# Attention with bias: adding and taking the row maximum in one VectorE instruction, and another order of matmuls in the product with v

## The chip, the cores and the metric

The kernel runs on one core of a Trainium2 chip (trn2), whose engines are TensorE (PE), VectorE (DVE), ScalarE (ACT), GpSimd (POOL) and the DMA engines, fed here by SyncE's queue (SP). Each engine works through a queue of its own in order and waits on semaphores that other engines raise. The metric is the device time of one execution in microseconds. All data are fp32.

## The reference, cut to what matters

The program computes four layers on an image of 256 x 256 positions and 128 channels. Each layer is `x = x + layer(group_norm(x))`. The change lies in the first of them, an attention along the rows of the image with 4 heads of 32 channels:

```python
mu = jnp.mean(z_ij, axis=-1, keepdims=True)
var = jnp.var(z_ij, axis=-1, keepdims=True)
z = (z_ij - mu) * jax.lax.rsqrt(var + LN_EPS) * ln_gamma + ln_beta
q = heads(z @ Wq)
k = heads(z @ Wk)
v = heads(z @ Wv)
bias = z @ Wb
g = jax.nn.sigmoid(heads(z @ Wg))
scores = jnp.einsum('bijhd,bikhd->bijkh', q, k) / np.sqrt(C_HIDDEN)
scores = scores + bias[:, None]
a = jax.nn.softmax(scores, axis=-2)
o = jnp.einsum('bijkh,bikhd->bijhd', a, v)
o = (g * o).reshape(b, n, n, HC)
return o @ Wout
```

So for each of the 256 image rows and each head there is a 256 x 256 matrix of scores (queries by keys). The same bias, which depends on query, key and head but not on the row, is added to each of them, and the softmax runs over the keys. The other layers are a selective scan over 65536 positions (by far the longest), a Fourier layer and a gated recurrence.

## The kernel before

`program` calls the layers one after another; each waits for what the one before has left in DRAM. `layer0` first normalises x (lines 110 to 142), leaves z and the bias in DRAM, and then calls `attention` (line 147), which the change edits.

`attention` works in blocks of 2048 positions, that is 8 rows of the image, 32 blocks in all. A block has 16 **units**: a unit is one row with two of the four heads (`u`, with `hp = u % 2` for the pair of heads), 512 units in all. The whole bias stays in SBUF (line 162). For one unit the steps are these:

- `scores` (line 201): four matmuls on PE (line 207), two heads times two halves of the queries, into the PSUM tile `l0b_sc`, of 128 partitions (queries) by 2 heads by 2 halves by 256 keys, which has two buffers. The heads lie in different groups of 32 partitions of q and k, and the loop has the halves outside and the heads inside. Then DVE adds the bias to all 1024 columns in one instruction (line 215), which leaves the sum in `l0b_e` in SBUF (four buffers), and takes the negated maximum over the keys for each of the four pieces in a second one (line 222) into `l0b_top`.
- `exps` (line 224): four exponentials on ACT (line 228), one for each piece, with the negated maximum as bias and the sum over the keys as accumulator output `l0b_den`; the reciprocal of the four sums on DVE (line 231); and the multiplication of the whole tile by it on POOL (line 232).
- `transposes` (line 234): eight transposes on PE (line 240), which bring the keys onto the partitions, four for each half of the keys, into `l0b_tp0` and `l0b_tp1`; ACT copies the first half to `l0b_at0` (line 243), DVE the second to `l0b_at1` (line 245).
- `product` (line 247): four matmuls on PE (line 254), two heads times two halves of the keys, which accumulate over the halves into `l0b_op`. Each head writes 32 partitions of its own. The loop has the heads outside and the halves inside.
- `gate` (line 264), once for two units: DVE multiplies by the gate (line 268).
- `out` (line 277), once for four units: a matmul on PE (line 281), then on DVE the addition of x (line 282) and the statistics for the next group norm (line 283).
- `project` (line 181), sixteen times for a block: the matmuls for k, q, v and the gate of the next block (lines 188 and 193), with a copy on DVE (lines 191 and 195) or ACT (lines 197 and 199).

A matmul of fp32 appears in the profile as two MATMUL instructions, a transpose as one.

The order of the work on all engines is written out by hand (`tc.manual_schedule()`, line 288): the loop runs over `u`, and each turn issues the steps of different units:

```python
if u + 2 < N:
    scores(u + 2)
if u + 1 < N:
    exps(u + 1)
if u < N:
    transposes(u)
if 5 <= i and b + 1 < NB:
    project(b + 1, i - 5)
if 1 <= u <= N:
    product(u - 1)
```

In each turn DVE's queue therefore holds, in this order: the gate (every second turn), the addition and maximum of unit u + 2, the reciprocal of unit u + 1, the copy of the transposes of unit u, and then the copies and additions of `project` and `out`, where there are any. The turns 0 to 4 of a block have no projection. The loads of z and x for the next block go through SP's queue (line 176), as does the store of a finished block (line 285).

Of the kernel before, what the change touches and what calls it, by code (L numbers as in the profile page):

```python
# [11 lines left out]
AF = mybir.ActivationFunctionType  # L12
ALU = mybir.AluOpType
AX = mybir.AxisListType
# [132 lines left out]
def attention(c, x, x1, zs, bs, w, stats):  # L147
# [3 lines left out]
    tc, nc = c.tc, c.nc  # L151
# [4 lines left out]
    with ExitStack() as a:  # L156
# [5 lines left out]
        bias = one.tile([P, NH, 2, S], F32, name="l0b_bias")  # L162
# [38 lines left out]
        def scores(u):  # L201
            k, r, hp = blocks[u // UB], u % UB // 2, u % 2
            sc = ps2.tile([P, 2, 2, S], F32, name="l0b_sc")
            for jt in range(2):
                for h in range(2):
                    hs = slice(32 * (2 * hp + h), 32 * (2 * hp + h) + 32)
                    nc.tensor.matmul(  # L207
                        sc[:, h, jt],
                        k["q"][hs, bass.ds(r * S + jt * P, P)],
                        k["k"][hs, bass.ts(r, S)],  # L210
                        start=True,
                        stop=True,
                    )
            e = es[u] = wk.tile([P, 4, S], F32, name="l0b_e", bufs=4)
            nc.vector.tensor_tensor(  # L215
                e,
                sc.rearrange("p h j k -> p (h j) k"),
                bias[:, 2 * hp : 2 * hp + 2].rearrange("p h j k -> p (h j) k"),
                ALU.add,
            )  # L220
            top = tops[u] = wk.tile([P, 4], F32, name="l0b_top")
            nc.vector.tensor_reduce(top, e, AX.X, ALU.max, negate=True)

        def exps(u):
            e, top = es[u], tops.pop(u)
            den = wk.tile([P, 4], F32, name="l0b_den")
            for i in range(4):
                nc.scalar.activation(  # L228
                    e[:, i], e[:, i], AF.Exp, bias=top[:, i : i + 1], accum_out=den[:, i : i + 1]
                )  # L230
            nc.vector.reciprocal(den, den)  # L231
            nc.gpsimd.tensor_tensor(e, e, den[:, :, None].to_broadcast([P, 4, S]), ALU.mult)  # L232
# [14 lines left out]
        def product(u):  # L247
            k, r, hp = blocks[u // UB], u % UB // 2, u % 2
            if hp == 0:
                ops[u // 2] = ps1.tile([P, S], F32, name="l0b_op")  # L250
            for h in range(2):
                hs = slice(32 * (2 * hp + h), 32 * (2 * hp + h) + 32)
                for kt in range(2):
                    nc.tensor.matmul(
                        ops[u // 2][hs],
                        k["v"][:, 2 * r + kt, hs],
                        ats[u, kt][:, h],
                        start=kt == 0,
                        stop=kt == 1,
                    )  # L260
            for kt in range(2):
                del ats[u, kt]
# [27 lines left out]
        for i in range(UB):  # L290
            project(0, i)
        scores(0)
        scores(1)
        exps(0)
        for u in range(N + 3):
            b, i = divmod(u, UB)
            if u >= 3 and u % 2 == 1:
                gate((u - 3) // 2)
            if i == 4 and b + 1 < NB:
                load_block(b + 1)  # L300
# [10 lines that stand above are left out]
            if u >= 5 and (u - 5) % 4 == 0:  # L311
                out((u - 5) // 4)
            if 5 <= i < 10 and b + 1 < NB:
                project(b + 1, i + 6)
# [1152 lines left out]
```

## Time and profile before

| | |
|---|---|
| time before, median of 3 runs (lowest, highest) | 35963.57 us (35957.72, 35963.6) |
| the profiled execution's own time | 35973.5 us |
| its span, first to last instruction | 35971.7 us |
| mean granted clock of TensorE in the span | 0.908 |
| busy in the span: PE, DVE, ACT, POOL | 83%, 89%, 63%, 74% |
| scores of the first unit start, of the last unit end, about | 805.7 us, 3490 us |

The page comes from one profiled execution. Engines are PE (matmuls), PEld (loading of weights), DVE, ACT, POOL and SP. A line such as `L215 DVE TENSOR_TENSOR` names the line of the kernel and the engine; behind it stand the tile written and, after the arrow, the tiles read. In a group of instructions follow the shapes, the number of instructions, the busy time in us and the mean duration of one in ns, and behind a second bar the idle time of the engine just before them, with what ended it. In the timeline each line has the start in us, the busy time in us, engine, line and operation, and in brackets the idle time before it. A table of stretches gives, for a window of time, each engine's busy time, the clock that PE was granted (1.00 is full), the share of the DMA engines in use and the bytes moved. In the list of waits a line says which engine and line waited for which, for how long in total, how often, and the longest. Matmuls are pipelined and their ends are modelled.

### The profile page before, as it was taken

The page shows a single profiled execution, that of the slowest core. Times are in us where ns is not written, and L with a number is a line of the kernel's source. Part 1 is how long each engine was busy: PE and PEld are TensorE (multiplying, and loading weights), DVE is VectorE, ACT ScalarE, POOL GpSimd, SP SyncE. Part 2 cuts the span into 40 slices and gives each one's busy share as a digit, 9 for nine tenths or more (in the row PEclk, how much of TensorE's full clock was granted, in tenths as well). Part 3 has the DMA queues.
Part 4 walks back from the last instruction along what each step waited for, and adds up shares of the span by engine and source line. Part 5 has one row for each costly group of instructions (what it writes and reads, how often), then busy time and mean ns, then how long its engine had stood idle before and what let it go on. Part 6 is the DMA issues. An engine that isn't in the chain of part 4 may idle for free. (4 is left out here: it accounts for less than half of the span.)

```text
span 35971.7 us, 251006 instructions
## 1 busy us (share of the span) xinstructions
PE 29891.5 (83%) x72562; PEld 12305.1 (34%) x72562; DVE 31866.8 (89%) x21006; ACT 22790.4 (63%) x47086; POOL 26745.5 (74%) x6540
## 2 busy tenths in 40 slices
PE   7888978888888888888888888888888887777988
PEld 1444433333333333333333333333333332223444
DVE  5777989999999999999999999999999998542599
ACT  2555567777777777777777777777777775332476
POOL 1333069999999999999999999999999997210000
PEclk8999989999999999999999999999999998889887
DMA  3111655555555554555555555555555556765211
GB/s 120 39 39 40 150 177 191 191 191 191 191 191 191 191 190 191 191 191 191 196 201 201 201 201 201 201 202 201 201 201 201 201 202 177 147 152 142 73 34 33
DMA packets 2480963, 5947.46 MB, mean 165 GB/s; under 512 B 1412999, under 2 KB 1694360, under 8 KB 1891286
## 3 DMA queue, kind: packets, MB, share of 16 engines
q1 hardware_dynamic: 2479574, 5931.39, 46.6%
q8 instruction: 572, 9.37, 0.1%
q14 instruction: 817, 6.69, 0.1%
HBM read 5238.41 MB, written 692.58 MB: 165 GB/s over the span
## 5 line engine op out<-in xcount | busy, mean ns | idle before, releaser
L651 DVE TENSOR_TENSOR_SCAN l1b_h<-l1b_da,l1b_state,l1b_db 128x1024 f32<-128x1024 f32 x8192 | 18792.8, 2336 | 598.1 <-ACT l1b_db L640 586.8
L666 POOL TENSOR_TENSOR l1b_hc<-l1b_h,l1b_cc 128x2048 f32<-128x2048 f32 x4096 | 18452.2, 4530 | 326.4 <-DVE l1b_h L651 321.0
L685 PE MATMUL l1b_y<-l1b_hc,ident 128*128 128x512 f32 x32768 | 16055.9, 639 | 1122.0 <-POOL l1b_hc L666 1121.9
L636 ACT ACTIVATE l1b_da<-l1b_dl,l_A 128x512 f32<-128x512 f32 (+1 forms) x16384 | 11297.0, 690 | 3153.0 <-DVE l1b_h L651 2845.2
L685 PEld LDWEIGHTS l1b_y<-l1b_hc,ident 128*128 128x128 f32 x32768 | 6525.3, 205 | 10692.9 <-issue 8161.7
L618 POOL TENSOR_TENSOR l1b_db<-l1b_bb,l1b_dus 128x2048 f32<-128x2048 f32 x1536 | 6969.5, 4537 | 1244.8 <-DMA l1b_bb<-l1b_bc 1244.8
L618 DVE TENSOR_TENSOR l1b_db<-l1b_bb,l1b_du 128x2048 f32<-128x2048 f32 x2048 | 4658.3, 2275 | 35.2
L640 ACT ACTIVATE l1b_db<-l1b_state,l1b_db,l1b_af 128x1 f32<-128x1 f32 x8192 | 3047.5, 372 | 0.0
L557 PE MATMUL l1b_mm<-l1b_xd,l_dtw 41*128 41x512 f32 x2048 | 1372.6, 755 | 1706.9 <-ACT l1b_dus L607 1701.2
L583 PE MATMUL l1b_mm<-l1b_tail,ident 128*128 128x512 f32 x2048 | 1293.9, 718 | 1387.1 <-ACT l1b_tail L577 1387.1
L662 ACT COPY l1b_state<-l1b_h 128x4 f32<-128x4 f32 x4095 | 790.3, 193 | 2433.0 <-DVE l1b_h L651 2432.9
L232 POOL TENSOR_TENSOR l0b_e<-l0b_e,l0b_den 128x1024 f32<-128x1024 f32 x512 | 969.8, 1894 | 1777.6 <-DVE l0b_den L231 1461.3
L869 POOL TENSOR_TENSOR l1c_y<-l1c_y,l1c_sz 128x512 f32<-128x512 f32 x256 | 369.8, 1468 | 1346.0 <-ACT l1c_y L866 1345.7
L583 PE MATMUL l1b_mm<-l1b_relu,ident 128*128 128x512 f32 x2048 | 1308.5, 728 | 0.0
L557 PEld LDWEIGHTS l1b_mm<-l1b_xd,l_dtw 41*128 41x128 f32 x2048 | 337.6, 206 | 2521.3 <-ACT l1b_dus L607 2124.2
L618 DVE TENSOR_TENSOR l1b_db<-l1b_bb,l1b_mm 128x2048 f32<-128x2048 f32 x512 | 1171.5, 2288 | 18.2 <-ACT l1b_dus L607 0.7
L607 ACT COPY l1b_dus<-l1b_mm 128x512 f32<-128x512 f32 x512 | 300.2, 586 | 1388.2 <-DVE l1b_db L618 1387.8
L228 ACT ACTIVATE l0b_e<-l0b_e,l0b_top 128x256 f32<-128x256 f32 x2048 | 1014.4, 497 | 209.6 <-DVE l0b_den L231 192.6
L399 DVE SCALAR_TENSOR_TENSOR l1a_mm<-l1a_xi,l1a_each,l1a_mm 128x512 f32<-128x512 f32 x1408 | 1046.0, 755 | 58.5 <-issue 12.7
L583 PEld LDWEIGHTS l1b_mm<-l1b_tail,ident 128*128 128x128 f32 x2048 | 377.3, 207 | 2057.7 <-ACT l1b_tail L577 1813.3
L525 PE MATMUL l1b_du<-l1b_xc,l_xproj 128*40 128x512 f32 x2048 | 981.5, 602 | 62.5 <-DMA l_ds<-in_l_ds 58.4
L215 DVE TENSOR_TENSOR l0b_e<-l0b_sc,l0b_bias 128x1024 f32<-128x1024 f32 x512 | 625.4, 1221 | 369.2 <-PE l0b_sc L207 365.9
(253 smaller groups left out, 30461.1 us busy)
## 6 DMA issues: line engine op xcount, KB each, us to landing
l1b_bb<-l1b_bc SPq DMA_DIRECT2D x2048, 1024.0 KB
l1b_cc<-l1b_bc SPq DMA_DIRECT2D x2048, 1024.0 KB
l_y<-l1b_yo SPq DMA_DIRECT2D x256, 1024.0 KB
l1b_xc<-l_xc SPq DMA_DIRECT2D x128, 1024.0 KB
l1b_xc<-l_xct SPq DMA_DIRECT2D x128, 1024.0 KB
l1b_yo<-l_y SPq DMA_DIRECT2D x128, 1024.0 KB
l_xc<-l1a_o SPq DMA_DIRECT2D x64, 1024.0 KB
l_xct<-l1a_ot SPq DMA_DIRECT2D x16, 4096.0 KB
```

The costliest lines, as they stand in the source:

```text
L228: nc.scalar.activation(e[:, i], e[:, i], AF.Exp, bias=top[:, i : i + 1], accum_out=den[:, i : i + 1])
L232: nc.gpsimd.tensor_tensor(e, e, den[:, :, None].to_broadcast([P, 4, S]), ALU.mult)
L399: nc.vector.scalar_tensor_tensor(mm, xis[i][:, r + dy : r + dy + 2, dx : dx + S], each[:, dh, tap : tap + 1], mm, ALU.mult, ALU.add,)
L525: nc.tensor.matmul(du1[:40], w["xproj"][:, dh, k, :], blocks[ch][0][:, dh, cols(ch)], start=dh == 0, stop=dh == 1,)
L557: nc.tensor.matmul(mm, w["dt"][:, chunks[ch][0], dh * P : dh * P + P], xds[ch % 3][0:41], start=True, stop=True,)
L583: nc.tensor.matmul(mm, c.ident, part, start=i == 0, stop=i == 1)
L618: eng.tensor_tensor(db, bbs[g // 2], du[:, None, :].to_broadcast([P, G, CH]), ALU.mult)
L636: nc.scalar.activation(da[:, o + lo : o + hi], dl[:, lo:hi], AF.Exp, scale=w["A"][:, k, dh, n : n + 1])
L640: nc.scalar.activation(first, states[k][:, dh, two : two + 1], AF.Identity, scale=af[:, two : two + 1], bias=first,)
L651: nc.vector.tensor_tensor_scan(h_, a_, d_, states[k][:, dh, one : one + 1], ALU.mult, ALU.add)
L666: nc.gpsimd.tensor_tensor(hc, hs[g], ccs[g // 2], ALU.mult)
L685: nc.tensor.matmul(ys[j % 2], c.ident, hc[:, i], start=False, stop=j // 2 * G + i == 15)
```

## The change

Two things change, both in `attention`.

First, in `scores` the addition over 1024 columns and the maximum over the same are replaced with four instructions of 256 columns, one for each piece (head and half of the queries). Each computes `(scores + bias) * -1`, writes it to `l0b_e`, and writes the minimum of what it wrote, over the keys and started at 3.0e38, to a column of `l0b_top`. The tile thus holds the negated sum, and `l0b_top` still the negated maximum. In `exps` the exponential takes a scale of -1, so that it computes exp(sum - maximum) as before.

Second, in `product` the two loops change places: the halves of the keys are now outside and the heads inside, so that the first half's matmuls of both heads are issued ahead of the second half's.

```diff
             e = es[u] = wk.tile([P, 4, S], F32, name="l0b_e", bufs=4)
-            nc.vector.tensor_tensor(
-                e,
-                sc.rearrange("p h j k -> p (h j) k"),
-                bias[:, 2 * hp : 2 * hp + 2].rearrange("p h j k -> p (h j) k"),
-                ALU.add,
-            )
             top = tops[u] = wk.tile([P, 4], F32, name="l0b_top")
-            nc.vector.tensor_reduce(top, e, AX.X, ALU.max, negate=True)
+            for i in range(4):
+                nc.vector.tensor_tensor_reduce(
+                    e[:, i],
+                    sc[:, i // 2, i % 2],
+                    bias[:, 2 * hp + i // 2, i % 2],
+                    -1.0,
+                    3.0e38,
+                    ALU.add,
+                    ALU.min,
+                    accum_out=top[:, i : i + 1],
+                )
 
         def exps(u):
             e, top = es[u], tops.pop(u)
             den = wk.tile([P, 4], F32, name="l0b_den")
             for i in range(4):
                 nc.scalar.activation(
-                    e[:, i], e[:, i], AF.Exp, bias=top[:, i : i + 1], accum_out=den[:, i : i + 1]
+                    e[:, i],
+                    e[:, i],
+                    AF.Exp,
+                    scale=-1.0,
+                    bias=top[:, i : i + 1],
+                    accum_out=den[:, i : i + 1],
                 )
...
-            for h in range(2):
-                hs = slice(32 * (2 * hp + h), 32 * (2 * hp + h) + 32)
-                for kt in range(2):
+            for kt in range(2):
+                for h in range(2):
+                    hs = slice(32 * (2 * hp + h), 32 * (2 * hp + h) + 32)
                     nc.tensor.matmul(
                         ops[u // 2][hs],
                         k["v"][:, 2 * r + kt, hs],
```

## The prediction

> **What bounds the kernel now.** I first read the busy time by stage, to see how much of the run the change can touch.
>
> ```profile
> core 0: us, PE busy (x) PEld busy (x) DVE busy (x) ACT busy (x) POOL busy (x), PEclk, DMA share, GB/s
> 805.70:3500.00 2694.30, 2327.62 (x14279) 1295.46 (x14278) 1997.59 (x2805) 1479.66 (x4858) 969.84 (x512) 0.95 0.10 36
> ```
>
> All instructions of the diff run in this row, the attention stage (times in us; behind each engine's busy time its number of instructions): 2694 us of 35972, 7.5%. What follows it needs its result and is not edited, so the forecast is the stage's change. In the stage no engine is full: PE 86%, DVE 74%. PE idles 2694.3 - 2327.6 = 366.7 us. The waits of that window say for what (total, times, longest):
>
> ```profile
> POOL l0b_e L232 <- DVE l0b_den L231: 1461.3, 406, 63.0
> ...
> PE l0b_tp L240 <- POOL l0b_e L232: 253.2, 195, 3.7
> ```
>
> Two thirds of PE's idle time is the transposes waiting for POOL's multiplication by 1/den, in 195 of 512 units, 1.30 us each; and POOL in turn waits for the reciprocal on DVE. Groups of the same window add waits of PE for DVE's copies: L193 48.6 (x) and 28.8 (v), L281 30.7 (k), 108 us in all. The timeline of two units shows why the reciprocal is late:
>
> ```profile
> 2002.57 1.21 DVE L215 TENSOR_TENSOR l0b_e<-l0b_sc,l0b_bias 128x1024 f32<-128x1024 f32 x1
> 2002.93 0.59 ACT L243 COPY l0b_at<-l0b_tp 128x512 f32<-128x512 f32 x1 [3.10 <-PE l0b_tp L240]
> ...
> 2003.21 1.06 PE L254 MATMUL l0b_op<-l0b_at,l0b_v 128*32 128x256 f32 x8
> 2003.81 1.22 DVE L222 TENSOR_REDUCE l0b_top<-l0b_e 128x4 f32<-128x1024 f32 x1
> ...
> 2004.20 1.13 PE L207 MATMUL l0b_sc<-l0b_k,l0b_q 32*128 32x256 f32 x8
> 2004.94 0.17 DVE L231 RECIPROCAL l0b_den<-l0b_den 128x4 f32<-128x4 f32 x1
> 2005.03 0.66 DVE L245 COPY l0b_at<-l0b_tp 128x512 f32<-128x512 f32 x1
> ...
> 2005.61 0.41 DVE L268 SCALAR_TENSOR_TENSOR l0b_gated<-l0b_g,l0b_op 128x256 f32<-128x256 f32 x1
> ...
> 2005.93 1.22 DVE L215 TENSOR_TENSOR l0b_e<-l0b_sc,l0b_bias 128x1024 f32<-128x1024 f32 x1
> ```
>
> ACT sat idle for 3.10 us until 2002.93, so the exponentials that the reciprocal at 2004.94 needs had ended by 1999.83. The reciprocal stood in DVE's queue behind the addition and maximum of the *next* unit (2002.57 to 2004.94). POOL starts at 2005.26 for 1.89 us, and PE, done with the scores at 5.33, waits 1.87 us for it until 2007.20. In the other unit of the pair the transposes follow the scores at once.
>
> The third thing is PE's clock. Stretches of 3.4 us around these waits:
>
> ```profile
> 2003.90:2007.30 3.40, 1.53 (x13) 0.78 (x10) 3.37 (x6) 2.08 (x8) 1.89 (x1) 1.00 0.99 311
> 2007.30:2010.70 3.40, 3.40 (x16) 1.96 (x16) 1.88 (x3) 2.38 (x9) 1.90 (x1) 0.51 1.01 424
> 2014.20:2017.60 3.40, 1.78 (x16) 1.33 (x15) 3.37 (x6) 2.25 (x9) 1.90 (x1) 1.00 0.00 0
> 2017.60:2021.00 3.40, 3.40 (x12) 0.95 (x10) 1.66 (x4) 0.42 (x1) 1.89 (x1) 0.50 0.00 0
> 2044.90:2048.30 3.40, 2.33 (x6) 0.74 (x8) 1.62 (x3) 0.04 (x1) 1.09 (x1) 1.00 0.00 0
> 2048.30:2051.70 3.40, 3.40 (x24) 2.05 (x26) 2.33 (x2) 3.40 (x11) 0.00 (x0) 1.00 0.00 0
> ```
>
> A stretch with PE busy for 1.53 or 1.78 us is followed by one at half clock; after 2.33 us the clock stays. The stage's mean of 0.95 thus stands for 0.05 x 2694 = 135 us of lost PE time (rounding +-13).
>
> [...] No DVE row here has such a read; on ACT the trace has it (L228, 188 ns behind each exponential), and DVE's early start it shows: L268 at 2005.61 took 0.41, the next began at 2005.93.[...]
>
> **The change, part by part.** *Removed*, per unit: the addition (1.22) and the maximum (1.22). From the timeline they hold DVE from 2002.57 to 2004.94: 2.37 us.
>
> *Added*: four fused instructions of 256 elements, PSUM plus SBUF. Main part: L268 has the same width and sources, 0.41 us; behind it the next starts 0.32 after (2005.61 to 2005.93). Accumulator read: no row; nearest is the tiny reciprocal, whose successor starts 0.09 after it (2004.94 to 2005.03). So 0.41 each and 4 x 0.41 = 1.64, a saving of 0.73. Ends: the read hidden wholly, 4 x 0.33 = 1.32, saving 1.05; nothing overlapping, 4 x (0.41 + 0.17) = 2.32, saving 0.05; half rate as in the scan L651 (2336 ns against 1221 for 1024, so +0.28 for 256), 4 x 0.69 = 2.76, *costing* 0.39. I take 0.41[...].
>
> On the path: the waits for POOL shorten by the saving, as the chain addition-maximum-reciprocal-POOL-transposes is serial: 195 x 0.73 = 142 us (their mean of 1.30 is well above 0.73). PE's 108 us for DVE's copies shorten too, since they stand behind the same instructions; at most 108, I take 65. In the other units PE is the limit and the saving is worth nothing. Clock: 1.53 + 0.73 = 2.26 and 1.78 + 0.73 = 2.51 are near or above the 2.33 that keeps full speed, so most half-clock stretches go; of 135 us I take 80, since part of that time lies under a wait already counted. Sum 142 + 65 + 80 = 287 us. What is late next is still POOL: 1.87 - 0.73 = 1.14 us remain.
>
> *New holds*: the scores' PSUM tile is now free after 1.64 us instead of 1.2; it has two buffers and is wanted two units on (2010.85 against 2003.8), so 0. Each fused instruction signals by itself; behind it in DVE's queue stand the reciprocal, the copy of the transposes and the gate, all earlier than now. No DMA is moved, and SP's and POOL's queues keep their order.
>
> *Exponentials*: an immediate scale of -1 for an immediate 1: 0. They may start after the first row of four, on an engine 55% busy: 0.
>
> *Product order*: 8 matmuls take 1.06 us (2003.21). L240's 8 of half the width take 1.09, so 256 wide one after another would be near 1.7: the heads already run in pairs. The new order is the one L207 has (1.13 for 8). If pairing broke, 0.8 x 512 = 410 us would be lost, which L207 excludes; not waiting for the second half of the keys could gain at most what the loads of L254 wait for L245, 39 us in the stage. Taken: 0.
>
> **Sum.** The profiled execution took 35973.5 us (span 35971.7): 35973.5 - 287 = 35686.5. The median of the runs is 9.9 lower, so 35677.
>
> **Rivals.** *The read is not hidden* (0.58 each, 2.32): saving 0.05, 10 to 25 us, no change: about 35955. For it: no DVE accumulator read is in the trace. Against: ACT's 188 ns read costs no more than its overlap. *Part of the way* (0.50 to 0.56 each, or half-clock stretches that stay): 100 to 180 us, about 35820. *Slower: [...]*, as L651 does: 2.76 us, +0.39 in every second unit, 256 x 0.39 = 100 us: 36064.[...] It decides from 0.59 us per fused instruction (2.37 / 4). *The change does nothing*, because PE is the limit: against it stand the 253 us.
>
> **How the numbers follow.** The forecast 0.62 (its own range 35590 to 35780), part of the way 0.12, unhidden 0.08, two cycles 0.18. About 0.2% (72 us) is what a measurement tells from no change. Faster 0.74, same 0.08, slower 0.18. The range from 35590 (read hidden, 1.05 saved: about 370 us) to 36000 leaves out the two-cycle case and the little below.
>
> **What would show it.** DVE's four rows from first start to reciprocal near 1.64 us; waits of L240 for POOL from 253 to some 110 us; clock 0.95 to 0.98; the rows of L254 unchanged. I am wrong if a fused instruction takes over 0.55 us from start to start, if POOL then waits for the exponentials, or if the clock stays at 0.95.

## The result, and the profile after

The changed kernel takes **35586.94 us** (median of 4 runs, 35581.59 to 35590.76) against 35963.58 for the kernel before: a ratio of 0.9895, 95% interval 0.9878 to 0.9912, or 377 us less. The forecast was 287 less: the sign and the place were right, the size was too small by 90, and the time lies 3 us below the low end of the range. The profiled execution took 35581.59 us, its span 35579.7.

First the attention stage by time, here from its first scores to its last (us, busy us of each engine, clock of TensorE):

```profile
core 0: us, PE busy (x) PEld busy (x) DVE busy (x) ACT busy (x) POOL busy (x), PEclk, DMA share, GB/s
...
803.50:3107.70 2304.20, 2181.32 (x14219) 1238.98 (x14220) 1527.50 (x5861) 1432.54 (x4845) 964.25 (x510) 1.00 0.11 43
```

Before, the first and the last scores lay 2683.2 us apart; now it is 2304.2, so all of the 377 us is in the stage. PE is busy for 95% of it (2181.3 us, where it was 2319.8), and the clock is at 1.00 where it was 0.95.

The waits in the same stretch as in the prediction, 805.70 to 3500.00 (total, times, longest):

```profile
POOL l0b_e L242 <- DVE l0b_den L241: 764.6, 322, 61.0
...
PE l0b_tp L250 <- POOL l0b_e L242: 74.7, 109, 1.6
...
PE l0b_mm L193 <- DVE l0b_x L292: 48.6, 62, 0.8
```

The transposes' wait for POOL fell from 253.2 to 74.7 us. Of the 108 us that PE waited for DVE's copies, the part for x (48.6) is as it was, and those for v (28.8) and k (30.7) are gone. The groups of the stage show the new instruction (busy us, mean ns, then idle time before it):

```profile
L218 DVE CUSTOM_DVE_ANT_0 l0b_e<-l0b_sc,l0b_bias 128x256 f32<-128x256 f32 x2048 | 745.5, 420 | 418.9 <-PE l0b_sc L207 415.5
...
L218 DVE DVE_READ_ACCUMULATOR2_ANT l0b_top<- 128x1 f32 x2048 | 170.1, 83 | 0.0
```

So an accumulating instruction of DVE is two here: the trace has 420 ns for the main one and 83 ns for the read. What matters is where the read lies, and that only the timeline shows:

```profile
2002.36 0.43 DVE L218 CUSTOM_DVE_ANT_0 l0b_e<-l0b_sc,l0b_bias 128x256 f32<-128x256 f32 x1
2002.71 0.08 DVE L218 DVE_READ_ACCUMULATOR2_ANT l0b_top<- 128x1 f32 x1
2002.71 0.42 DVE L218 CUSTOM_DVE_ANT_0 l0b_e<-l0b_sc,l0b_bias 128x256 f32<-128x256 f32 x1
...
2003.40 0.42 DVE L218 CUSTOM_DVE_ANT_0 l0b_e<-l0b_sc,l0b_bias 128x256 f32<-128x256 f32 x1
2003.74 0.08 DVE L218 DVE_READ_ACCUMULATOR2_ANT l0b_top<- 128x1 f32 x1
2003.74 0.17 DVE L241 RECIPROCAL l0b_den<-l0b_den 128x4 f32<-128x4 f32 x1
...
2004.06 1.89 POOL L242 TENSOR_TENSOR l0b_e<-l0b_e,l0b_den 128x1024 f32<-128x1024 f32 x1 [2.89 <-DVE l0b_den L241]
```

Each read starts in the same moment as the next main instruction (2002.71 and 2002.71; the last one beside the reciprocal, 2003.74); in the whole trace 1955 of the 2048 reads start together with another instruction of DVE. The read adds next to nothing to the chain: from one main instruction to the next it is 0.345 us (median), where L268, of the same width and without a read, was followed after 0.32. From the first start to the reciprocal it is 1.38 us where it was 2.37, a saving of **0.99 us**; the prediction had 1.64 and 0.73.

And the stretches of 3.4 us around these instructions:

```profile
2001.00:2004.40 3.40, 3.40 (x27) 2.62 (x28) 3.06 (x12) 1.39 (x5) 0.51 (x2) 1.00 0.00 0
2004.40:2007.80 3.40, 3.40 (x23) 1.75 (x20) 1.11 (x5) 1.49 (x6) 1.56 (x1) 1.00 0.02 5
...
2014.60:2018.00 3.40, 2.62 (x10) 0.71 (x6) 1.92 (x3) 0.00 (x0) 1.40 (x1) 1.00 0.00 0
```

PE is no longer half idle in any of them, and the clock column stays at 1.00.

**A sum to be tested.** The stage lasts as long as TensorE is busy and idle in it. If its idle time is its waits (for POOL's multiplication and for DVE's copies), and if work done at half clock takes twice as long (in the kernel before, L240's transposes start 109 ns apart at clock 1.00 and 213 ns apart at 0.50), a kernel's difference from before should be the difference in these waits plus half of the difference in the time at half clock (the time in which the trace's record of TensorE's clock says 0.50; the record has the two values 1.00 and 0.50, and in the kernel before all but one of its 2402 entries last a multiple of 3.41 us). Added up between first and last scores, that time is 286.8 us before, 13.7 after; the 13.7 are the first stretch of the stage. Waits: 74.7 + 48.6 - 361.3 = -238. Clock: (13.7 - 286.8) / 2 = -137. Together -375, against a stage that is 379 us shorter. The second term has a figure of its own: PE's busy time fell by 138 us (2319.8 - 2181.3). The prediction gave the same two terms 142 + 65 = 207 and 80.

### The profile page after: what moved, and what is told of

The parts are those of the page before. It is cut to its first block, busy times and chain, and to the rows that moved or that the text cites. A ratio compares the mean times of both kernels' runs of the same rounds, so it can differ in the third digit from the quotient of the medians.

```text
span 35579.7 us, 254592 instructions
## 1 busy us (share of the span) xinstructions
PE 29747.9 (84%) x72562; PEld 12259.8 (34%) x72562; DVE 31402.5 (88%) x24078; ACT 22740.5 (64%) x47086; POOL 26737.3 (75%) x6540
## 5 line engine op out<-in xcount | busy, mean ns | idle before, releaser
L661 DVE TENSOR_TENSOR_SCAN l1b_h<-l1b_da,l1b_state,l1b_db 128x1024 f32<-128x1024 f32 x8192 | 18792.9, 2336 | 596.4 <-ACT l1b_db L650 585.7
L218 DVE CUSTOM_DVE_ANT_0 l0b_e<-l0b_sc,l0b_bias 128x256 f32<-128x256 f32 x2048 | 745.5, 420 | 418.9 <-PE l0b_sc L207 415.5
```

The lines of the kernel that those rows point to most:

```text
L661: nc.vector.tensor_tensor_scan(h_, a_, d_, states[k][:, dh, one : one + 1], ALU.mult, ALU.add)
```

## The experiments

The theory: what delays the stage is what the reciprocal and the copies stand behind in DVE's queue; the waits follow from it, and the clock is a term of its own that is added to them. The rivals are stated with each run. Each ratio is against runs of the kernel before on the same chip.

**The two parts apart.** First the new order in the product alone, on the kernel before:

```diff
-            for h in range(2):
-                hs = slice(32 * (2 * hp + h), 32 * (2 * hp + h) + 32)
-                for kt in range(2):
+            for kt in range(2):
+                for h in range(2):
+                    hs = slice(32 * (2 * hp + h), 32 * (2 * hp + h) + 32)
```

> The kernel before with the new order of matmuls in the product alone; addition and maximum stay two instructions. My theory: the heads already ran in pairs, so nothing beyond 6 ns per unit, 3 us in all: 35960 +-10. The rival, that not waiting for the second half of the keys is where part of the unforecast 90 us came from, has at least 40 us: 35920 or less.

Measured: 35937.47 us (35930.61 to 35944.49), ratio 0.9993, interval 0.9985 to 1.0001: 27 us less than before, with an interval that includes no change, though its 13 runs all lie below those of the kernel before on the same chip (35957.54 and up). The waits did not move:

```profile
PE l0b_tp L240 <- POOL l0b_e L232: 254.5, 196, 3.7
...
PE l0b_mm L193 <- DVE l0b_x L282: 48.6, 62, 0.8
...
PE l0b_mm L281 <- DVE l0b_k L195: 30.6, 32, 1.0
...
PE l0b_mm L193 <- DVE l0b_v L191: 29.0, 31, 0.9
```

The time at half clock fell from 286.8 to 231.5 us, worth 28. That the heads already ran in pairs the trace of the kernel before shows: the matmuls of L254 start two at a time, 13 ns apart (7 ns in the changed kernel's L264), and each pair 216 ns after the last. The order thus saves no wait; fewer stretches fall to half clock (60 instead of 76, without the first and the last 30 us). Why these 16 don't, isn't settled: in the kernel before 45 half-clock stretches follow one with PE 52 to 53% busy, and 8 stretches after such a one keep the clock; with the new order it is 29 and 18.

Then the fused instruction alone, with the old order in the product.

> The changed kernel with the old order of matmuls in the product: the fused instruction alone. My theory: the whole gain, 35587 +-10, since the product order is worth nothing. The rival that the product order carries part of the gain: 35620 or more.

Measured: 35587.01 us (35585.58 to 35589.34), ratio 0.9896, interval 0.9881 to 0.9911: the whole gain. Here 20.0 us of half clock are left, all in one stretch at the start of the stage, so the order of the product has nothing to win any more. The product's matmuls, on which the prediction wanted no change, in this kernel (old order) and in the changed one:

```profile
L264 PE MATMUL l0b_op<-l0b_at,l0b_v 128*32 128x256 f32 x4096 | 545.9, 386 | 0.0
```

```profile
L264 PE MATMUL l0b_op<-l0b_at,l0b_v 128*32 128x256 f32 x4096 | 541.0, 385 | 0.0
```

The same mean. In the kernel before it was 422 ns, with a tenth of the stage at half clock: 385 ns at clock 1.00 and 634 at 0.50.

**Do the exponentials gain from starting early?** The four fused instructions in reverse order, so that the first exponential waits for the last of them:

```diff
-            for i in range(4):
+            for i in (3, 2, 1, 0):
                 nc.vector.tensor_tensor_reduce(
```

> The changed kernel with its four fused instructions in the reverse order, so that the first exponential has to wait for the last of them, as it did for the maximum before. Theory (the exponentials' earlier start is worth nothing): within 12 us of the changed kernel, 35575 to 35600. Rival (part of the gain is that ScalarE may start after the first quarter): the first exponential comes up to 3 x 0.345 = 1.03 us later, and the time rises to 35640 or more.

Measured: 35587.48 us (35580.93 to 35589.03), ratio 0.9897, interval 0.9882 to 0.9912. The time is that of the changed kernel; the rival falls. The early start is there in the changed kernel: in 194 of the 512 units the first exponential starts before the unit's last accumulator read has ended, by up to 1.00 us; the time shows nothing of it.

**How the time follows the delay of the reciprocal.** A memset on DVE between the fused instructions and the reciprocal, of a tile that nobody reads, gives part of the saved time back:

```diff
+        pad = one.tile([P, 330], F32, name="l0b_pad")
...
+            nc.vector.memset(pad, 0.0)

         def exps(u):
```

> The changed kernel with a VectorE memset of 330 columns of a spare tile behind the four fused instructions of each unit, about 0.25 us of the queue, so that the stretch from the first fused instruction to the reciprocal takes the 1.64 us that the prediction had instead of 1.38. Theory 1, the mis-sized term is the saving per unit (the accumulator read costs nothing) and the clock: the two halves of the miss part here. If the prediction's other terms were right, 35677; if the clock term was too small by some 60 us, 35587 + 195 x 0.25 = 35636 or a little more, clock 0.98 or above in the stage. Rival, the gain comes from something else than DVE's time (exponentials that start after one piece of four): 35587 still.

> The changed kernel with a VectorE memset of 650 columns between the fused instructions and the reciprocal: from the two pads run so far, first start to reciprocal about 1.38 + 0.15 + 0.52 = 2.05 us. Theory (the gain has two terms, waits in proportion to that time and a clock that stays full as long as the stretches around the waits are busy enough): waits about half way between the short pad (178 us) and before (361), some 270, so 35656 + 92 = 35750 if the clock stays full, and up to 35880 if it falls back; the half-clock time tells which. Rival (one slope for all): 35656 + 308 x 0.33 / 0.65 = 35812, with half-clock time about half of the 287 us before.

> The same with a memset of 1250 columns, about 1.02 us, which gives back all that fusing saved on DVE's queue (2.37 us again), while the scores' tile is free early and the exponentials may start after one piece. Theory: all of the gain goes, 35960 +-60, half-clock stretches come back, the stage's clock about 0.95. Rival, the early start of the exponentials or the earlier release of the scores' tile is worth something by itself: clearly below 35900.

The first tells whether the prediction's other terms were right once its term for the fused instructions is. Of the middle one a timeline:

```profile
2002.53 0.42 DVE L219 CUSTOM_DVE_ANT_0 l0b_e<-l0b_sc,l0b_bias 128x256 f32<-128x256 f32 x1
...
2003.91 0.08 DVE L219 DVE_READ_ACCUMULATOR2_ANT l0b_top<- 128x1 f32 x1
2004.07 0.60 DVE L229 MEMSET l0b_pad<- 128x650 f32 x1
2004.59 0.12 DVE L243 RECIPROCAL l0b_den<-l0b_den 128x4 f32<-128x4 f32 x1
```

It is 2.06 us from the first start to the reciprocal here; over all units the median is 2.07. The memset doesn't start together with the last read, as the reciprocal did, but 0.16 us later (2003.91 to 2004.07); with 330 and 1250 columns the median of that gap is 0.10 and 0.29 us, which I had not counted. From the memset's own start to the reciprocal's it is 0.25, 0.52 and 1.02 us in the timelines of the three runs. The five points:

| columns of the memset | first start to reciprocal, median us | PE's waits, us | half clock, us | worked out | stage, measured | time, us |
|---|---|---|---|---|---|---|
| none (changed kernel) | 1.38 | 123.3 | 13.7 | -375 | -379.0 | 35586.94 |
| 330 | 1.73 | 178.1 | 20.0 | -317 | -307.8 | 35655.82 (ratio 0.9915, 0.9901 to 0.9928) |
| 650 | 2.07 | 264.9 | 98.8 | -190 | -187.7 | 35773.88 (0.9949, 0.9935 to 0.9964) |
| the kernel before | 2.39 | 361.3 | 286.8 | 0 | 0 | 35963.58 |
| 1250 | 2.69 | 428.8 | 446.1 | +147 | +135.9 | 36104.04 (1.0040, 1.0027 to 1.0052) |

"Worked out" is the difference of the waits plus half that of the half clock, against before. It meets each stage within 12 us. The time isn't straight in the delay: by the column of the stage (the times come from chips on which the kernel before differed by up to 10 us), the first 0.35 us cost 71, the next 0.34 cost 120, the next 0.32 cost 188. The waits grow by 55, 87, 96 and 67 us from row to row; half clock does not move at first and then comes in (14, 20, 99, 287, 446 us).

With 330 columns the delay is near the prediction's (1.73 against 1.64), and yet the time is 21 us below the forecast. The two terms part here: the waits are shorter by 183 us where the prediction had 207, and the half clock, of which only the first stretch of the stage is left, is worth 133 where it had 80. So even with the prediction's own figure for the fused instructions its clock term was too small. With 1250 the delay is longer than before, and so is the time; I expected about the time of before, because I took the memset for 1.02 us more where, with the gap before it, it came to 1.31. This is the place of the prediction's slower rival (2.76 us, forecast +100): 2.69 costs +141. Its direction is right, and its turning point, 2.37 us, fits the points on both sides; its price was one of waits alone (they grew by 67) and had left out the clock, 80 of the 147.

**Is the clock a term of its own?** The kernel before, with four transposes of the identity ahead of the transposes of each odd unit, where PE waits. They write what the real ones overwrite:

```diff
                 tp = ps1.tile([P, 2, 2, P], F32, name=f"l0b_tp{kt}")
+                if kt == 0 and u % 2 == 1:
+                    for d in range(4):
+                        nc.tensor.transpose(tp[:, d // 2, d % 2], c.ident, c.ident)
```

> The kernel before, with four transposes of the identity into the tile tp0 (overwritten at once by the real ones) issued ahead of the transposes of every odd unit, where TensorE waits for GpSimd. Theory (the half clock is a term of its own, set by how little TensorE does in a stretch): the 4 x 0.136 = 0.55 us fit into the waits, of 1.30 us[...] and take most of the 287 us at half clock away, worth 143 at most; units without a wait pay 61 x 0.55 = 33. So 35964 - 80 to 110 = 35855 to 35885, with half-clock time under 60 us. Rival (the clock follows the waits, and a faster TensorE only waits longer for GpSimd): the clock rises, the waits for GpSimd grow as much, and the time is within 20 us of before, or up to 140 longer where the transposes are not hidden.

Measured: 35854.33 us (35849.32 to 35858.35), ratio 0.9970, interval 0.9958 to 0.9982. A kernel that only does more work is 109 us faster. One turn, and its stage:

```profile
2000.78 0.66 PE L240 MATMUL l0b_tp<-ident 128*128 128x128 f32 x4
2001.61 1.09 PE L243 MATMUL l0b_tp<-ident,l0b_e 128*128 128x128 f32 x8 [0.17 <-POOL l0b_e L232]
```

```profile
1500.00:2500.00 1000.00, 915.54 (x5920) 530.58 (x5919) 770.18 (x1085) 572.08 (x1877) 372.86 (x197) 0.99 0.10 39
```

The four stand where PE would have idled, 0.17 us of the wait remain, and the clock is 0.99, where the kernel before had 0.95 in the same stretch. Half clock fell from 286.8 to 54.1 us, worth 116. The sum: waits 220.2 - 361.3 = -141, the added transposes 1024 x 0.136 = +139, clock -116: -118, against a measured -108.3. The rival, that a faster PE only waits longer, falls: the waits plus the added work are as long as the waits were. Four added fp32 transposes in each odd unit thus kept the clock at 0.99, though 11 stretches in which PE was 62 to 63% busy were still followed by half clock.

**Which units matter?** The fused instruction in even units alone, and in odd ones alone (the others keep addition and maximum, and a scale of 1):

```diff
-            for i in range(4):
+            if u % 2 == 0:
+                for i in range(4):
...
+            else:
+                nc.vector.tensor_tensor(...)
+                nc.vector.tensor_reduce(top, e, AX.X, ALU.max, negate=True)
```

> The changed kernel with the fused instruction in even units alone; odd units keep addition and maximum. Theory (only the addition and maximum that stand ahead of a waited-for reciprocal count; transposes wait in odd units, and the reciprocal of an odd unit stands behind the addition and maximum of the next, even unit): nearly the whole gain, 35590 to 35650. Rival (what counts is VectorE's load over all units): half of the gain, about 35775.

> The changed kernel with the fused instruction in odd units alone; even units keep addition and maximum. Theory (as for the even units): little of the gain, 35880 to 35965, with the waits for GpSimd still near 250 us. Rival (VectorE's load over all units): half of the gain, about 35775.

Measured: 35840.25 us (35838.43 to 35853.76), ratio 0.9967, interval 0.9954 to 0.9979, for even; 35833.31 (35800.72 to 35839.7), 0.9961, 0.9948 to 0.9974, for odd. My theory of the even units falls: each gives a third of the gain, where I had forecast nearly all for the even and little for the odd ones. But they give different things. Waits with even units fused:

```profile
PE l0b_tp L259 <- POOL l0b_e L251: 118.8, 171, 2.4
...
PE l0b_mm L300 <- DVE l0b_k L195: 90.0, 93, 1.0
...
PE l0b_mm L193 <- DVE l0b_x L301: 48.6, 62, 0.8
...
PE l0b_mm L193 <- DVE l0b_v L191: 28.9, 31, 0.9
```

and with odd units fused:

```profile
PE l0b_tp L259 <- POOL l0b_e L251: 252.0, 193, 3.5
...
PE l0b_mm L193 <- DVE l0b_x L301: 48.6, 62, 0.8
```

The even units' instructions set the waits for POOL in odd units: the reciprocal of an odd unit stands behind them in the queue. The odd units' instructions set those for the copies of k and v: these stand, in an odd turn, behind the odd unit's instructions, and with those fused the two rows are gone. But the row of POOL (253 to 119) hides a move, which a count of the trace's waits by unit shows. Before, 249 us of it lay in odd units and 4 in even ones. With the even units fused, 10 are left in odd units, and 109 lie in even ones, whose reciprocal still stands behind an unfused odd unit. And PE meets the late copy of k at the output projection more often (93 times instead of 32), so that this row rises from 30.7 to 90.0. Of the 240 us won in odd units, 105 come back as waits for POOL in even units and 59 as waits for k. Half clock is 194.0 and 177.5 us. Worked out -121 and -115, measured -119.5 and -126.7. The two gains add up to 253; the other 124 us come only with both. The rival (half of the gain each, 35775) falls too.

**Would the place in the queue alone do?** The reciprocal put ahead of the next unit's addition and maximum, first in the kernel before, then in the changed one:

```diff
-            if u + 2 < N:
-                scores(u + 2)
             if u + 1 < N:
                 exps(u + 1)
+            if u + 2 < N:
+                scores(u + 2)
```

> The kernel before, with the exponentials and reciprocal of unit u+1 issued ahead of the scores, addition and maximum of unit u+2; nothing fused. Theory (what delays the reciprocal is its place in VectorE's queue behind the addition and maximum of the next unit): the reciprocal of the waited-for units comes up to 2.4 us earlier, the 253 us of waits for GpSimd fall under 100, the half clock goes with them: 35600 to 35750. Rival (the length of the chain addition, maximum, exponentials, reciprocal counts, not the place in the queue; and the additions now stand behind a reciprocal that waits for the exponentials): 35950 or slower than before.

> The changed kernel with the exponentials and reciprocal of unit u+1 issued ahead of the scores and fused instructions of unit u+2. From what that order cost the kernel before (358 us; VectorE's reciprocal waited for ScalarE, with the additions and the copies behind it): slower than the changed kernel, 35700 to 35900. Rival (with the chain 0.99 us shorter the exponentials are done in time, so that the remaining 75 us of waits for GpSimd go): 35500 to 35570.

Measured: 36321.11 us (36312.44 to 36325.99), ratio 1.0099, interval 1.0084 to 1.0114, on the kernel before, 358 us slower. In its timeline:

```profile
2009.63 0.18 DVE L231 RECIPROCAL l0b_den<-l0b_den 128x4 f32<-128x4 f32 x1 [3.88 <-ACT l0b_e L228]
2009.72 1.19 DVE L215 TENSOR_TENSOR l0b_e<-l0b_sc,l0b_bias 128x1024 f32<-128x1024 f32 x1
```

and its waits:

```profile
DVE l0b_den L231 <- ACT l0b_e L228: 767.7, 448, 4.8
...
PE l0b_mm L281 <- DVE l0b_k L195: 196.3, 93, 3.2
...
PE l0b_tp L240 <- POOL l0b_e L232: 121.9, 123, 3.7
```

The reciprocal waits for the exponentials, and DVE's whole queue with it: the next unit's addition starts 0.09 us after it, and the copies come late. PE's waits for POOL are halved, but those for the copies rise by more, and half clock goes to 771.0 us. Waits +92, clock +242: +334, against +357.7. My theory of the place in the queue falls in this form.

On the changed kernel the same edit **gains**: 35539.46 us (35535.69 to 35542.83), ratio 0.9884, interval 0.9868 to 0.9901; beside it on the same chip the kernel with the reversed order, equal to the changed one, took 35587.48. Here I had expected a loss; the time lies where the rival had it.

```profile
DVE l0b_den L241 <- ACT l0b_e L233: 511.4, 329, 3.9
...
PE l0b_mm L193 <- DVE l0b_x L292: 48.6, 62, 0.8
...
PE l0b_mm L291 <- DVE l0b_k L195: 28.5, 62, 1.0
...
PE l0b_tp L250 <- POOL l0b_e L242: 5.2, 10, 1.8
```

DVE still waits for the exponentials, 511 us, so they are not always done in time, as the rival had supposed; but DVE has the time to wait: PE's waits for POOL are 5.2, those for k 28.5. Worked out -412, measured -423.6. That it is the 1 us shorter work per unit that makes room is argued from these rows, not shown by a run of its own.

**What is left, and a faster version.** POOL's multiplication in two, the keys that the first transposes read ahead of the others:

```diff
-            nc.gpsimd.tensor_tensor(e, e, den[:, :, None].to_broadcast([P, 4, S]), ALU.mult)
+            for kt in range(2):
+                ks = bass.ts(kt, P)
+                nc.gpsimd.tensor_tensor(
+                    e[:, :, ks], e[:, :, ks], den[:, :, None].to_broadcast([P, 4, P]), ALU.mult
+                )
```

> The changed kernel with GpSimd's multiplication in two, first the 128 keys that the first four transposes read, then the rest. Theory (what is left of TensorE's waits for GpSimd is the length of the multiplication): the first half ends about 0.95 us earlier, and most of the 75 us of waits go: 35520 to 35560. Rival (each GpSimd instruction has a fixed cost of some tenths of a us, and the second half comes later than the whole did; or TensorE is the limit anyway): 35580 to 35650.

Measured: 35543.98 us (35540.96 to 35549.84), ratio 0.9886, interval 0.9871 to 0.9900.

```profile
L244 POOL TENSOR_TENSOR l0b_e<-l0b_e,l0b_den 128x512 f32<-128x512 f32 x1024 | 1042.9, 1039 | 1289.6 <-DVE l0b_den L241 736.7 <-PE l0b_mm L193 526.8 <-PE l0b_tp L254 26.1
```

```profile
PE l0b_mm L193 <- DVE l0b_x L296: 48.6, 62, 0.8
...
PE l0b_tp L254 <- POOL l0b_e L244: 24.6, 100, 0.8
```

Two halves take 2 x 1.04 = 2.08 us where the whole took 1.89, 0.19 more, but the first is done 0.85 us earlier, and 50 of the 75 us of waits go. This and the exponentials first both beat the changed kernel, by 43 and 47 us. That is little, 0.12 and 0.13%, and the intervals of the ratios to the kernel before overlap; but none of the four runs of either comes near those of the reversed order on the same chip (35580.93 to 35589.03). The two together were not tried; they reach for the same waits.

## Why the prediction was right in kind and too small

- **What bounds the stage**: right. PE's waits for POOL were the largest part of the idle time, and they fell most.
- **"4 x 0.41 = 1.64, a saving of 0.73"**: the first step that failed. The prediction had seen main instructions start 0.32 us apart (2005.61 to 2005.93), and added 0.09 for the accumulator read, an estimate, because the trace of before had none on DVE. Measured is 0.345 from start to start, the read wholly beside the next instruction: 1.38 us, near its low end (1.32). The mechanism, a shorter queue ahead of the reciprocal, was right; the size of the saving was not.
- **"195 x 0.73 = 142 us"**: measured 178.5. With the true saving the product would have been 195 x 0.99 = 193, but 56 of the 195 waits were shorter than 0.99 us, which their mean of 1.30 hid; when each wait loses 0.99 us at most, they lose 179.
- **"At most 108, I take 65"**: measured 59.5, and near by luck: the 65 had no working, and at about the saving that the prediction had (the run with 330 columns) the copies give 44. The waits for x stayed whole.
- **"In the other units PE is the limit and the saving is worth nothing"**: wrong. Fusing the odd units alone gains 130 us, through the copies and the clock, and without it two thirds of what the even units win come back as waits for POOL and for k.
- **"Of 135 us I take 80, since part of that time lies under a wait already counted"**: the second step that failed, and with 57 us the larger error. Waits and clock don't overlap, they add: the half clock comes in the stretch after the half-idle one, in which PE is busy and each matmul takes longer (L254: 634 ns where it takes 385 at full clock). The prediction's own rows showed PE busy for 3.40 of 3.40 us in both of its stretches at half clock. Nearly all of it went, (286.8 - 13.7) / 2 = 137 us. The run with added transposes shows it as a term of its own (116 us for no shorter chain), and the run with 330 columns shows it gone at 0.66 us of saving already (133 us).
- The errors add up: 287 + 36 (waits for POOL) - 6 (copies) + 57 (clock) = 374, against 375 from the sum above and 377 measured.
- **Product order 0, exponentials' start 0, new holds 0**: right beside the fused instruction (35587.01 without the new order, 35587.48 with the exponentials held). Alone the order is worth perhaps 27 us through the clock, a way that the prediction had not seen. The 410 us for broken pairs don't follow from the prediction's own figures (1.7 - 1.06 = 0.64 us a unit, or 330; the 1.7 was an estimate, which the 216 ns from pair to pair bear out, 8 x 0.216 = 1.73); nothing rests on them.
- **The rivals**: read not hidden, part of the way, the slower one ("two cycles"), nothing: none came. What spoke against the first was ACT in the trace of before: with a read of 188 ns behind each exponential, the next still starts 492 ns (median) after one of 497. That the fused instruction might run as slowly as L651 was an estimate, taken from its 2336 ns for 1024 elements; measured is 420 ns for 256. The price of the slower one was too low for the same reason as the gain.

## What to carry to other kernels

When TensorE sets the pace and idles in short, regular waits, as here, price a change as shorter waits **plus** half of the time at half clock that these waits cause, and count both from the trace; here they added (238 and 137 us, of a stage 379 us shorter). Look for each waiter at what stands ahead of the instruction it waits for in the other engine's queue, unit by unit: here two kinds of units held up different waiters, and mending one alone brought 164 of 240 us back as other waits. An edit of the order in a queue should be tried again after the work in it has shrunk; here it changed its sign.

## What the runs showed of the hardware

- The accumulator read of DVE (83 ns) started together with the next fused instruction or the reciprocal and added 0.02 us at most (0.345 against 0.32 us from start to start); a memset behind it started 0.10 to 0.29 us later. An accumulating fp32 instruction of 256 columns from PSUM and SBUF took 420 ns and started 345 ns after the one before.
- The clock of TensorE fell from 1.00 to 0.50 after stretches of 3.41 us in which it was about half busy. The busy share alone doesn't decide: in the kernel before, all 31 stretches under 50% were followed by half clock, and of 53 at 52 to 53% 45 were; in the run with 650 columns 19 at 55 to 57% were too, and in the run with added transposes 11 of those at 62 to 63%. What else decides stays open.
- Work without use on TensorE, placed in such waits, made a kernel 0.3% faster (0.9970, 0.9958 to 0.9982).
